# Turning the layer-1 weights through one ring of five buffers

## The chip, the cores and the metric

The kernel runs on one core of a Trainium2 chip. The metric is the device time of one execution, in microseconds. Before the change it is 4451.68 us, the median of three runs (4451.40 to 4455.35).

A core has a tensor engine (PE), a vector engine (DVE), a scalar engine (ACT), GpSimd (POOL) and a sync engine (SP). Each takes its instructions in a fixed order. Here SP issues plain loads and stores, and POOL issues gathers (indirect DMAs).

## The reference

The program is a two-layer model on `x` of 32 batches x 512 nodes x 256 features with an integer adjacency of 32 x 512 x 512. Each layer adds a graph step and then a feed-forward step to `x`:

```python
x = x + L0_gnn(layernorm(x), adj);  x = x + L0_ffn(layernorm(x))
x = x + L1_gnn(layernorm(x), adj);  x = x + L1_ffn(layernorm(x))
```

The feed-forward of layer 0 mixes a "tropical" product with a classical one:

```python
trop = max_d(x[:, None, :] + Wt[None]) + bt      # then piecewise linear
fused = g * trop + (1 - g) * gelu(x @ Wc + bc);  out = fused @ Wd + bd
```

The feed-forward of layer 1 projects the nodes softly onto 64 slices per head, runs a two-directional state-space mixer over the slices, and spreads the result back:

```python
fx = x @ W_fx.T;  sw = softmax((x @ W_x.T @ W_slice.T + b_slice) / temp)
zxbcdt = st @ hy_in_w.T;  ...  yg = yg * rsqrt(mean(yg ** 2)) * hy_norm_w
ot = yg @ hy_out_w.T;  out = spread(ot, sw) @ out_w.T + out_b
```

All weights of layer 1 come as rows (output by input). The kernel needs several of them turned, with the input dimension on the partitions.

## The kernel before

**Layer 0** (`layer0_sorted`, lines 98 to 704) handles the batches in four segments of eight. In a segment, 32 tiles of 128 rows make eight groups of four tiles. For a group, `sums` (L546 to L610) gathers the rows of four tiles (`xs`), transposes them (`xsp`, L577, into two PSUM banks tagged "tp"), and computes the tropical product by gathers. A row's result is the maximum over a short list of candidate features, each of which needs one gathered row of a table:

- the first candidate is gathered into `best` (L564), and ACT adds its value (L592);
- for tiles with more than eight candidates, DVE finds the list (`tops`, L585 to L589);
- each further candidate is a POOL gather of 512 KB (`rows`, L595) followed by a DVE maximum (L598). There are four `rows` buffers.

ACT then copies the transposed rows to `xnT` (L605). `mixed` (L613 to L643) does the classical half: per feature block the matmuls `clsp` and `gatep` (L623), ACT's functions `cls` and `gate` (L625), the transposes `tz` of `best` (L630), ACT's `acc` and `past` (L632, L636), and DVE's mixing (L637 to L641). `down` (L645 to L655) is the last matmul `po` (L652, 64 matmuls a group), a DVE addition and the store `x2s` by SP. The code interleaves the `mixed` of one group with the `sums` of the next.

In names such as `best_1_3` below, the first number is the group and the second the tile; for `clsp_0_5`, `tz_1_0` and the like, the group and the feature block. Group 7 is the last one of segment 2, groups 0, 1 and 2 are the first ones of segment 3. Pieces are called by their weight and row block: `in_0` is the first of `hy_in_w`.

**Layer 1** (`layer1_plain`, from L865) begins with a set-up that makes its turned weights. It is a Python generator: at each `yield` the program goes back to emitting layer-0 work. The set-up is thus interleaved with the last segment's feed-forwards, in the stretch from about 1849 to 2110 us of the profiled execution. A scheduler then settles the order of each engine from priorities and from its own estimates, and the engines run in that order. So the order in which the code is written and the order in which an engine runs it are not quite the same. A pool hands out buffers by tag: an instruction that needs a tile waits until the tile's earlier user is done.

The set-up before the change:

- `load_T` (L992 to L1004) takes a weight in pieces of 128 rows. For each, SP loads the piece into a raw buffer (L998), PE transposes its blocks of 128 columns into a "tp" PSUM bank (L1002), ACT copies the result into the turned weight (L1003). Raw buffers have one tag for each width with two buffers each. There are 21 pieces: `W_fx` 4 (256 columns, 128 KB each), `hy_in_w` 10 (512 columns, 256 KB each, the last one 16 rows), `hy_out_w` 4, `out_w` 2, `hy_fcD_w` 1. The "tp" banks are the same two that layer 0 uses for `xsp`.
- The norm weight is loaded (L1012), and DVE scales the turned `hy_out_w` (`hoT`) with it in four multiplications (L1014).
- `W_slice` is loaded twice and transposed (`twice_T`, L1016 to L1025); `W_x` (L1030), `b_x` (L1032) and `b_slice` (L1035) are loaded.
- Their products `wslp` (L1044), the scaled `wsl` (L1048), the bias row `bsl` (L1051 to L1055), its exponential `ebsl` (L1068), and bounds from the squares `wsl2` (L1060) follow.
- Then come the masks of batch 0 (L1073 to L1108): adjacency rows `ai` loaded by SP, `a` made by ACT, `maskp` transposed by PE.

Of the kernel before, what the change touches and what calls it, by code (L numbers as in the profile page):

```python
# [8 lines left out]
F32 = mybir.dt.float32  # L9
# [10 lines left out]
P = 128  # L20
N = 512
D = 256
# [842 lines left out]
def layer1_plain(tc, ident, eps, x2s, ranks, adj, w, out, over, ps):  # L865
# [3 lines left out]
    nc = tc.nc  # L869
# [31 lines left out]
    with ExitStack() as ctx:  # L901
# [3 lines left out]
        def ctile(name, shape):  # L905
            return cst.tile(shape, F32, tag=name, name=name)
# [6 lines left out]
        def psum(tag, name):  # L913
            return ps.tile([P, N], F32, tag=tag, name=name)
# [10 lines left out]
        with tc.tile_pool(name="raw0", bufs=1, side="right") as raw:  # L925
            prod = raw.tile([P, DC, AH, HO], F32, tag="prod", name="prod")
            norm2 = raw.tile([P, DC, 2, AH], F32, tag="norm2", name="norm2")
            for i, name in enumerate(("a_dst", "a_src")):
                dst = wa[:, :, AH * (HO + i) : AH * (HO + i + 1)]
# [51 lines left out]
        wfxT = ctile("wfxT", [P, DC, DI])  # L981
# [3 lines left out]
        inT = ctile("inT", [P, KC, DIN])  # L985
        hoT = ctile("hoT", [P, KC, DI])
        owT = ctile("owT", [P, KC, D])
        fcT = ctile("fcT", [P, KC, H])

        with tc.tile_pool(name="raw", bufs=2, side="right") as raw:  # L990

            def load_T(dst, src, name):  # L992

                R, Ccols = src.shape
                for r0 in range(0, R, P):
                    n = min(P, R - r0)
                    t = raw.tile([P, Ccols], F32, tag=f"raw{Ccols}", name=f"{name}_{r0}")
                    nc.sync.dma_start(t[:n], src[r0 : r0 + n, :])  # L998
                    pt = psum("tp", f"{name}p{r0}").rearrange("p (c r) -> p c r", r=P)
                    cs = Ccols // P  # L1000
                    for c in range(cs):
                        nc.tensor.transpose(pt[:, c, :n], t[:n, c * P : (c + 1) * P], ident[:n, :n])  # L1002
                    nc.scalar.copy(dst[:, :, r0 : r0 + n], pt[:, :cs, :n])  # L1003
                    yield  # L1004

            yield from load_T(wfxT, w["W_fx"], "wfx")
            yield from load_T(inT, w["hy_in_w"], "in")
            yield from load_T(hoT, w["hy_out_w"], "ho")
            yield from load_T(owT, w["out_w"], "ow")
            yield from load_T(fcT, w["hy_fcD_w"], "fc")  # L1010
            norm = raw.tile([P, KC], F32, tag="norm", name="norm")
            nc.sync.dma_start(norm, w["hy_norm_w"].rearrange("(c p) -> p c", p=P))  # L1012
            for c in range(KC):
                nc.vector.tensor_scalar_mul(hoT[:, c, :], hoT[:, c, :], norm[:, c : c + 1])  # L1014

            def twice_T(src, name):  # L1016

                R, Ccols = src.shape
                t = raw.tile([P, 2, Ccols], F32, tag="twice", name=name)
                for i in range(2):  # L1020
                    nc.sync.dma_start(t[:R, i, :], src)
                pt = psum("tp", f"{name}p")
                nc.tensor.transpose(pt[:, :R], t[:R].rearrange("p i c -> p (i c)"), ident[:R, :R])
                return pt


            wsT = raw.tile([P, G], F32, tag="wsT", name="wsT")
            nc.vector.tensor_copy(wsT, twice_T(w["W_slice"], "ws")[:, :G])
            wx = raw.tile([P, KC, D], F32, tag="wx", name="wx", bufs=1)
            nc.sync.dma_start(wx, w["W_x"].rearrange("(k p) d -> p k d", p=P))  # L1030
            bx = raw.tile([P, KC], F32, tag="bx", name="bx")
            nc.sync.dma_start(bx, w["b_x"].rearrange("(k p) -> p k", p=P))  # L1032
            bsl = raw.tile([1, H, G], F32, tag="bsl", name="bsl", bufs=1)
            bs = raw.tile([1, G], F32, tag="bs", name="bs")
            nc.sync.dma_start(bs, w["b_slice"].rearrange("(o n) -> o n", o=1))  # L1035
            for c in range(DC + 1):
                M = P if c < DC else 1
                for i in range(H // KC):

                    half = slice(i * C, (i + 1) * C)  # L1040
                    px = psum("mm", f"wslp{c}_{i}")
                    for k in range(KC):
                        lhs = wx[half, k, c * P : (c + 1) * P] if c < DC else bx[half, k : k + 1]
                        nc.tensor.matmul(px[:M, k * G : (k + 1) * G], lhs, wsT[half, :], start=True, stop=True)  # L1044
                    px = px[:M, : KC * G].rearrange("p (k g) -> p k g", k=KC)
                    rt = rtemp[:M, i :: H // KC].unsqueeze(2).to_broadcast([M, KC, G])
                    if c < DC:
                        nc.vector.tensor_mul(wsl[:, c, i :: H // KC, :], px, rt)  # L1048
                    else:
                        dst = bsl[:, i :: H // KC, :]  # L1050
                        nc.vector.tensor_add(dst, px, bs.unsqueeze(1).to_broadcast([1, KC, G]))  # L1051
                        nc.vector.tensor_mul(dst, dst, rt)
                yield
            wsl = wsl.rearrange("p c h g -> p c (h g)")
            nc.sync.dma_start(bsl_row.rearrange("(o n) -> o n", o=1), bsl.rearrange("p h g -> p (h g)"))  # L1055
            nc.sync.dma_start(ebsl, bsl_row.partition_broadcast(P))
            pn = psum("mm", "norm2s")
            for c in range(DC):
                sq = raw.tile([P, H * G], F32, tag="wsl2", name=f"wsl2_{c}")
                nc.vector.tensor_mul(sq, wsl[:, c, :], wsl[:, c, :])  # L1060
                nc.tensor.matmul(pn, ones, sq, start=c == 0, stop=c == DC - 1)
            most = raw.tile([P, 3], F32, tag="most", name="most")
            nc.vector.tensor_reduce(most[:, 0:1], pn, AX.X, ALU.max)
            nc.vector.tensor_reduce(most[:, 1:2], ebsl, AX.X, ALU.max)
            nc.vector.tensor_reduce(most[:, 2:3], ebsl, AX.X, ALU.min)
            for i, limit, op in ((0, SMALL_S, ALU.is_gt), (1, SMALL_B, ALU.is_gt), (2, -SMALL_B, ALU.is_lt)):
                nc.vector.tensor_scalar(over[:, 2 * AH + i : 2 * AH + i + 1], most[:, i : i + 1], limit, None, op)
            nc.scalar.activation(ebsl, ebsl, AF.Exp)  # L1068
# [1089 lines left out]
def tile_kernel(ctx, tc, ins, out):  # L2158
# [81 lines left out]
```

## Time and profile before

| | us |
|---|---|
| median of three runs | 4451.68 |
| lowest and highest run | 4451.40, 4455.35 |
| profiled execution, its own time | 4459.08 |
| span of the profiled execution | 4456.4 |
| PE busy (88% of the span) | 3922.0 |
| DVE busy (75%) | 3347.2 |
| ACT busy (51%) | 2291.6 |
| POOL busy (39%) | 1718.8 |

The mean granted TensorE clock is 0.948 of full speed. The profile is of one execution; times in microseconds count from the start of its span. In a line of waits, the numbers are the total, the times and the longest; in a timeline line, the start, the duration, the engine, the code line, the operation, the tiles written and read, and in brackets the idle time ahead of it with what ended it. "PE" rows are matmuls, "PEld" rows weight loads that overlap with them, "SPq" rows the DMA issues of SP.

### The profile page before, as it was taken

Reading aid. Unit: us, or ns where it says so; the run is one execution under the profiler, and the core shown is the slowest. Engines: PE = TensorE matmul, PEld = TensorE weight load, DVE = VectorE, ACT = ScalarE, POOL = GpSimd, SP = SyncE. Lnnn points to the kernel's source line nnn. Section 1 sums busy time; section 2 is a strip of 40 time slices with the busy share of each in tenths; the row PEclk is TensorE's granted clock in tenths of the full one; section 3 lists DMA queues with packets and bytes.
Section 4 is the critical chain, followed back from the end, with each engine's and each line's share of the span. In section 5 each row is a group of like instructions: output and inputs, shape, how many; then the busy total and the mean of one; then the engine's idle time right before and its main releaser. Section 6 shows DMA issues by size and latency. Waiting matters only on the chain.

```text
span 4456.4 us, 57911 instructions
## 1 busy us (share of the span) xinstructions
PE 3922.0 (88%) x20311; PEld 2470.6 (55%) x20311; DVE 3347.2 (75%) x7008; ACT 2291.6 (51%) x4756; POOL 1718.8 (39%) x2036
## 2 busy tenths in 40 slices
PE   5568898899988999888997899999999999999987
PEld 4454565566656656545554455555555555555555
DVE  6668887897788987877766777767677877778763
ACT  3345565566564665556654544544545444454433
POOL 2357644664446644454314232332222232332220
PEclk8679999999999999989998999999999999999998
DMA  5546543664436543564422111111111111111100
GB/s 133 160 144 223 190 130 122 210 200 139 156 117 213 187 147 129 162 201 167 138 81 67 36 53 57 56 48 58 51 43 42 53 55 55 58 48 58 41 15 16
DMA packets 235107, 474.21 MB, mean 106 GB/s; under 512 B 38299, under 2 KB 114075, under 8 KB 234804
## 3 DMA queue, kind: packets, MB, share of 16 engines
q0 software_dynamic: 98688, 315.94, 22.2%
q1 hardware_dynamic: 136116, 154.46, 11.0%
q8 instruction: 162, 2.65, 0.2%
q14 instruction: 141, 1.16, 0.1%
HBM read 413.16 MB, written 57.16 MB: 106 GB/s over the span
## 4 chain that ended last, share of the span: by engine, by line
DVE 34%; PE 32%; DMA 11%; issue 9%; POOL 9%; ACT 5%; SPq 0%; POOLq 0%; DVEq 0%; ACTq 0%
DVE att L1213 5%; DVE acc L637 4%; PE clsp L623 3%; PE avp L1249 3%; PE po L652 3%; PE gatep L623 3%; DMA rows<-table,xs 2%; PE yTp L1347 2%; DVE sw L1337 2%; DVE sw L1342 2%; DVE best L598 2%; DMA rows<-table,tops 2%; DVE sst L1340 2%; DMA best<-table,xs 2%; PE xp L1400 1%
## 5 line engine op out<-in xcount | busy, mean ns | idle before, releaser
L623 PE MATMUL clsp<-xnT,wc 128*128 128x512 f32 x1024 | 520.8, 627 | 49.7 <-ACT cls L625 37.6
L623 PE MATMUL gatep<-xnT,wg 128*128 128x512 f32 x1024 | 499.8, 607 | 10.5 <-ACT gate L625 7.7
L652 PE MATMUL po<-wd,acc 128*128 128x256 f32 x2048 | 455.4, 381 | 6.1 <-DVE acc L641 3.8
L1213 DVE SCALAR_TENSOR_TENSOR att<-own,other,mask 128x512 f32<-128x512 f32 x512 | 392.9, 796 | 79.0 <-DMA own<-ownd 79.0
L652 PEld LDWEIGHTS po<-wd,acc 128*128 128x128 f32 x2048 | 388.3, 191 | 72.1 <-issue 9.2
L598 DVE SCALAR_TENSOR_TENSOR best<-rows,xs,best 128x1024 f32<-128x1024 f32 x212 | 274.4, 1295 | 121.9 <-ACT best L592 76.4
L637 DVE SCALAR_TENSOR_TENSOR acc<-past,fld,acc 128x512 f32<-128x512 f32 x448 | 345.7, 775 | 24.9 <-ACT past L636 16.9
L632 ACT ACTIVATE acc<-tz,fld 128x512 f32<-128x512 f32 x256 | 198.8, 777 | 269.3 <-PE tz L630 240.1
L623 PEld LDWEIGHTS gatep<-xnT,wg 128*128 128x128 f32 x1024 | 196.0, 196 | 252.3 <-issue 197.9
L636 ACT ACTIVATE past<-tz,fld 128x512 f32<-128x512 f32 x448 | 291.4, 693 | 68.1 <-DVE acc L637 66.6
L1347 PE MATMUL yTp<-sw,x 128*128 128x512 f32 x512 | 264.6, 655 | 64.3 <-DVE sw L1342 59.6
L595 POOL DMA_INDIRECT rows<-table,xs x212 | 249.5, 1177 | 171.6 <-DVE best L598 119.0
L1249 PE MATMUL avp<-att,hv 128*32 128x512 f32 x2048 | 298.9, 607 | 5.6 <-DVE att L1213 5.6
L623 PEld LDWEIGHTS clsp<-xnT,wc 128*128 128x128 f32 x1024 | 181.5, 198 | 188.1 <-issue 111.8
L434 PE MATMUL pm<-h,adj 128*128 128x258 f32 (+1 forms) x1024 | 181.2, 324 | 99.9 <-DVE keep L427 33.7
L1300 POOL TENSOR_TENSOR mu<-mu,eps 128x16 f32<-128x16 f32 x32 | 111.6, 3487 | 391.1 <-DVE mu L1299 391.0
L1335 PE MATMUL lgp<-wsl,x4T 128*128 128x512 f32 x512 | 242.8, 613 | 15.7 <-ACT sw L1336 6.8
L1154 POOL DMA_INDIRECT x<-x2s,ranks x128 | 135.9, 1062 | 298.1 <-DVE att L1213 148.1
L625 ACT ACTIVATE gate<-gatep,fld 128x512 f32<-128x512 f32 x256 | 175.5, 685 | 142.6 <-PE gatep L623 123.8
L553 POOL DMA_INDIRECT xs<-rows_of,order x128 | 156.1, 1219 | 221.5 <-DVE acc L637 100.8
L1567 PE MATMUL outp<-v,swT 128*128 128x256 f32 x1024 | 227.6, 381 | 0.0
L625 ACT ACTIVATE cls<-clsp,fld 128x512 f32<-128x512 f32 x256 | 176.1, 688 | 93.9 <-PE clsp L623 55.6
(599 smaller groups left out, 8978.1 us busy)
## 6 DMA issues: line engine op xcount, KB each, us to landing
adj<-in_adj POOLq DMA_DIRECT2D x128, 256.0 KB
ai<-in_adj SPq DMA_DIRECT2D x128, 256.0 KB
own<-ownd SPq DMA_DIRECT2D x128, 256.0 KB
rows_of<-keep SPq DMA_DIRECT2D x32, 550.0 KB
x<-in_x SPq DMA_DIRECT2D x32, 512.0 KB
x2s<-xs SPq DMA_DIRECT2D x32, 512.0 KB
out<-x SPq DMA_DIRECT2D x32, 512.0 KB
rows<-table,xs POOLq DMA_INDIRECT x212
```

The costliest lines, as they stand in the source:

```text
L595: nc.gpsimd.indirect_dma_start(out=row, out_offset=None, in_=table, in_offset=bass.IndirectOffsetOnAxis(ap=idxs[:, k : k + 1].bitcast(U32) ...
L598: nc.vector.scalar_tensor_tensor(m, row, vals[:, k : k + 1], m, ALU.add, ALU.max)
L623: nc.tensor.matmul(pf, wf[:, c, f * P : (f + 1) * P], xnT[:, c, :], start=c == 0, stop=c == DC - 1)
L625: nc.scalar.activation(o, pf, fn, bias=fld[:, f, bf : bf + 1], scale=1.0 if fn == AF.Gelu else 0.5)
L636: nc.scalar.activation(r, z, AF.Relu, bias=fld[:, f, AT + b : AT + b + 1])
L637: nc.vector.scalar_tensor_tensor(y, r, fld[:, f, CH + b : CH + b + 1], y, ALU.mult, ALU.add)
L652: nc.tensor.matmul(po[:, i, :], acc[f][:, t * P : (t + 1) * P], wd[:, f, :], start=f == 0, stop=f == FC - 1)
L1213: nc.vector.scalar_tensor_tensor(e, own[h], other[:, j, h : h + 1], mask[:, j, :], ALU.max, ALU.mult)
L1249: nc.tensor.matmul(pv[p][k * HW : (k + 1) * HW, :], hv[:, j, h, e : e + HW], weighed[b, h, j], **ends)
L1335: nc.tensor.matmul(pf, xnT[:, c, t * P : (t + 1) * P], wsl[:, c, :], start=c == 0, stop=c == DC - 1)
L1347: nc.tensor.matmul(py, xn[:, t, c * P : (c + 1) * P], sw[:, t, :], start=t == 0, stop=t == NT - 1)
L1567: nc.tensor.matmul(po[:, :D], swT[:, k, t * P : (t + 1) * P], v[:, k, :], start=k == 0, stop=k == KC - 1)
```

## The change

The small operands `W_x`, `W_slice` (twice), `b_x` and `b_slice` are loaded first. The 21 pieces go through one tag, `piece`, of five buffers of 512 columns each. Before a piece is transposed, the load of the piece three places on is emitted, and three loads are emitted before the first transpose, followed by one more `yield`. The squares `wsl2` take their buffers from the same ring. The helper `twice_T` is written out in place. No operation is added or taken away.

In the order built for each engine the following has moved, between about 1840 and 2110 us; outside it, the order is the same:

- SP issues `W_x`, `W_slice`, `b_x`, `b_slice`, pieces 0 to 4, the norm weight, pieces 5 to 8, the store of group 6, pieces 9 to 20, then the store of group 7. Before, it was `W_fx` 0 and 1, `in_0` and `in_1`, the norm weight, the small operands, `W_fx` 2 and 3, the store of group 6, the remaining pieces, the store of group 7.
- On PE and ACT, `in_0` to `in_9`, `ho_0` to `ho_3` and `ow_0` stand in one stretch after the `xnT_0` copies; before, `in_0` stood before group 0's `xsp`, and the others were spread between the matmuls of `po_7`. `po_7` now follows them in one block, then `ow_1`; `fc`, the `W_slice` transpose and `wslp` come after the `xnT_1` copies.
- On ACT, the addition for `best_0_3` stands before the `xnT_0` copies.
- On DVE, the four multiplications of `hoT` by the norm stand between the searches that fill `tops_1_0`; before, they stood after them.
- On PE, `po_0` stands behind `tz_1_0` and `tz_1_1` of tile `best_1_3` and the mask transposes; before, it stood ahead of them.

```diff
-            def load_T(dst, src, name):
-                R, Ccols = src.shape
-                for r0 in range(0, R, P):
-                    n = min(P, R - r0)
-                    t = raw.tile([P, Ccols], F32, tag=f"raw{Ccols}", name=f"{name}_{r0}")
-                    nc.sync.dma_start(t[:n], src[r0 : r0 + n, :])
-                    pt = psum("tp", f"{name}p{r0}").rearrange("p (c r) -> p c r", r=P)
...
-                    nc.scalar.copy(dst[:, :, r0 : r0 + n], pt[:, :cs, :n])
-                    yield
-            yield from load_T(wfxT, w["W_fx"], "wfx")
-            yield from load_T(inT, w["hy_in_w"], "in")
...
+            wx = raw.tile([P, KC, D], F32, tag="wx", name="wx", bufs=1)
+            nc.sync.dma_start(wx, w["W_x"].rearrange("(k p) d -> p k d", p=P))
+            twice = raw.tile([P, 2, w["W_slice"].shape[1]], F32, tag="twice", name="ws", bufs=1)
+            for i in range(2):
+                nc.sync.dma_start(twice[:G, i, :], w["W_slice"])
+            bx = raw.tile([P, KC], F32, tag="bx", name="bx")
+            nc.sync.dma_start(bx, w["b_x"].rearrange("(k p) -> p k", p=P))
+            bs = raw.tile([1, G], F32, tag="bs", name="bs")
+            nc.sync.dma_start(bs, w["b_slice"].rearrange("(o n) -> o n", o=1))
+            pieces = [(dst, w[name], r0)
+                      for dst, name in ((wfxT, "W_fx"), (inT, "hy_in_w"), (hoT, "hy_out_w"), (owT, "out_w"),
+                                        (fcT, "hy_fcD_w"))
+                      for r0 in range(0, w[name].shape[0], P)]
+            def fetch(i):
+                _, src, r0 = pieces[i]
+                n = min(P, src.shape[0] - r0)
+                t = raw.tile([P, DI], F32, tag="piece", name=f"piece{i}", bufs=5)
+                nc.sync.dma_start(t[:n, : src.shape[1]], src[r0 : r0 + n, :])
+                return t
+            coming = [fetch(i) for i in range(3)]
+            yield
+            for i, (dst, src, r0) in enumerate(pieces):
+                if i + 3 < len(pieces):
+                    coming.append(fetch(i + 3))
+                n, cs = min(P, src.shape[0] - r0), src.shape[1] // P
+                pt = psum("tp", f"piecep{i}").rearrange("p (c r) -> p c r", r=P)
+                for c in range(cs):
+                    nc.tensor.transpose(pt[:, c, :n], coming[i][:n, c * P : (c + 1) * P], ident[:n, :n])
+                nc.scalar.copy(dst[:, :, r0 : r0 + n], pt[:, :cs, :n])
+                yield
             norm = raw.tile([P, KC], F32, tag="norm", name="norm")
             nc.sync.dma_start(norm, w["hy_norm_w"].rearrange("(c p) -> p c", p=P))
             for c in range(KC):
                 nc.vector.tensor_scalar_mul(hoT[:, c, :], hoT[:, c, :], norm[:, c : c + 1])
...
-                sq = raw.tile([P, H * G], F32, tag="wsl2", name=f"wsl2_{c}")
+                sq = raw.tile([P, H * G], F32, tag="piece", name=f"wsl2_{c}", bufs=5)
```

More of the change, by code (lines that the diff above doesn't have):

```diff
@@ L990, in layer1_plain @@
         with tc.tile_pool(name="raw", bufs=2, side="right") as raw:
-            def load_T(dst, src, name):
-                R, Ccols = src.shape
-                for r0 in range(0, R, P):
-                    n = min(P, R - r0)
-                    t = raw.tile([P, Ccols], F32, tag=f"raw{Ccols}", name=f"{name}_{r0}")
-                    nc.sync.dma_start(t[:n], src[r0 : r0 + n, :])
-                    pt = psum("tp", f"{name}p{r0}").rearrange("p (c r) -> p c r", r=P)
[L1000 to L1003, printed above, removed]
-                    yield
@@ L1006, in layer1_plain @@
-            yield from load_T(wfxT, w["W_fx"], "wfx")
-            yield from load_T(inT, w["hy_in_w"], "in")
-            yield from load_T(hoT, w["hy_out_w"], "ho")
-            yield from load_T(owT, w["out_w"], "ow")
-            yield from load_T(fcT, w["hy_fcD_w"], "fc")
+            wx = raw.tile([P, KC, D], F32, tag="wx", name="wx", bufs=1)
+            nc.sync.dma_start(wx, w["W_x"].rearrange("(k p) d -> p k d", p=P))
+            twice = raw.tile([P, 2, w["W_slice"].shape[1]], F32, tag="twice", name="ws", bufs=1)
@@ L1014, in layer1_plain @@
                 nc.vector.tensor_scalar_mul(hoT[:, c, :], hoT[:, c, :], norm[:, c : c + 1])
[L1016 to L1024, printed above, removed]
-            wsT = raw.tile([P, G], F32, tag="wsT", name="wsT")
[L1028 to L1032, printed above, removed]
+            pt = psum("tp", "wsp")
+            nc.tensor.transpose(pt[:, :G], twice[:G].rearrange("p i c -> p (i c)"), ident[:G, :G])
+            wsT = raw.tile([P, G], F32, tag="wsT", name="wsT")
+            nc.vector.tensor_copy(wsT, pt[:, :G])
             bsl = raw.tile([1, H, G], F32, tag="bsl", name="bsl", bufs=1)
-            bs = raw.tile([1, G], F32, tag="bs", name="bs")
-            nc.sync.dma_start(bs, w["b_slice"].rearrange("(o n) -> o n", o=1))
             for c in range(DC + 1):
```

## The prediction

> **What bounds the kernel now.** I read the page's busy times first, then the busy time by stretch around the edited code, then the waits of each engine there, the timeline of TensorE, and the chain that ended last. Page, part 1:
>
> ```profile
> PE 3922.0 (88%) x20311; PEld 2470.6 (55%) x20311; DVE 3347.2 (75%) x7008; ACT 2291.6 (51%) x4756; POOL 1718.8 (39%) x2036
> ```
>
> PE is the fullest engine, but that is an average. The edited code runs once, from 1849 us (its first load) to about 2010 us, beside the last feed-forwards of layer 0. By stretch:
>
> ```profile
> core 0: us, PE busy (x) PEld busy (x) DVE busy (x) ACT busy (x) POOL busy (x), PEclk, DMA share, GB/s
> 1895.00:1911.00 16.00, 14.91 (x50) 7.64 (x50) 16.00 (x19) 11.05 (x19) 11.26 (x10) 1.00 0.54 157
> 1911.00:1956.00 45.00, 33.88 (x140) 23.00 (x139) 28.45 (x41) 17.03 (x28) 20.36 (x18) 0.89 0.76 264
> 1956.00:2000.00 44.00, 39.22 (x145) 21.79 (x144) 33.73 (x52) 24.57 (x39) 20.26 (x20) 0.81 0.51 159
> 2000.00:2050.00 50.00, 42.44 (x154) 25.58 (x153) 42.65 (x56) 36.32 (x70) 26.87 (x22) 0.93 0.61 212
> ```
>
> In 1911 to 1956 no engine is full: PE idles 11.1 us of 45, DVE 16.5. This is where weight pieces are loaded and turned two at a time. SP's waits from 1845 to 1960, then DVE's waits from 1900 to 1960:
>
> ```profile
> SPq L998 <- PE inp L1002: 36.5, 8, 29.3
> SPq L998 <- DMA in<-in_L_ffn_hy_in_w: 15.3, 7, 4.1
> ```
>
> ```profile
> DVE hoT L1014 <- ACT hoT L1003: 11.1, 1, 11.1
> ```
>
> SP stood 29.3 us at one load, from 1882 to 1911, because both 512-wide buffers were full; then the loads came late. PE's timeline, and the chain that ended last:
>
> ```profile
> 1916.64 0.63 PE L1002 MATMUL inp<-ident,in 128*128 128x128 f32 x4 [1.92 <-DMA in<-in_L_ffn_hy_in_w]
> ...
> 1929.17 0.63 PE L1002 MATMUL inp<-ident,in 128*128 128x128 f32 x4 [2.91 <-DMA in<-in_L_ffn_hy_in_w]
> ...
> 1944.05 1.08 PE L1002 MATMUL hop<-ident,ho 128*128 128x128 f32 x4 [3.00 <-DMA ho<-in_L_ffn_hy_out_w]
> ```
>
> ```profile
> 1937.33 6.40 DMA rows<-table,tops
> 1943.77 8.70 issue
> 1952.69 0.93 POOL rows L595
> ```
>
> The chain shows what the late pieces cost. Rows for tile best_1_0 were gathered by 1943.8, but DVE stood at the norm scaling (L1014) until the last hoT copy, 1949.56. Its first maximum came at 1951.14, the next gather at 1952.69: the 8.70 us called issue. The edit can touch this, and nothing beyond 2110 us: the built order of each engine is the same there and before 1840 us.
>
> **What the Trainium skill says.** "PSUM — Partial Sum Buffer", Engine vs sequencer instructions, says that the queues of ScalarE, VectorE and GpSimdE are strict first in, first out. The trace agrees: DVE stood 11.1 us with rows for its next instruction there. "Perfetto Trace Analysis", Optimization Strategy, reads a repeated gap as possibly too few buffers for the next tile; SP's eight waits for inp agree. "DMA: Bandwidth & Descriptors", Issuing engines are not separate DMA queues, says that transfers from all issuers run on the same 16 engines and interleave: SP's pieces and POOL's gathers will compete. The trace has the share at 0.76 with both under way; it cannot show how a deeper ring divides it.
>
> **The change, part by part.** Instruction counts stay the same on every engine; only places and buffers change.
>
> *Small operands first.* W_x (512 KB), W_slice twice and the two biases go ahead of piece 0: five issues at the durations SP shows, 0.59 + 1.15 + 0.51 + 0.40, so piece 0 starts 2.7 to 3.1 us later. PE first stops for a piece at 1862.83 with a 4.36 us gap, and that gap is ACT's (its copy stands behind a layer-0 tile whose gather is late), so the delay fits under it: 0. If that gather were early it would cost up to 3.
>
> *Five buffers.* Load k now waits for the transposes of piece k-5. Pieces 0 to 3 are W_fx, turned at 1857 to 1881 as before, so pieces 5 to 8 (hy_in_w rows 1 to 4, 256 KB each) load at 1857 to 1882 rather than after 1881. That moves some 0.8 to 1 MB, 3 to 4 us of the 270 GB/s moved there, in among gathers. I put +1 (0 to +4). Layer 0's store x2s_6 stands behind pieces 7 and 8 on SP: at most 2.6 us later, with nobody waiting for it soon: 0.
>
> *The bunch.* hy_in_w piece 0 is no longer turned at 1881; fifteen pieces (in0 to in9, ho0 to ho3, ow0) now stand in one bunch on PE and ACT after the feed-forward's xsp transposes. Five are there at its start. The rest come five in flight; a load took 4.9, 5.3, 6.4, 6.6 and 5.7 us from issue to use before, so one each 1.1 to 1.3 us against 2.5 to 3 with two in flight. The bunch needs 15 x 0.6 = 9 us on PE and as much on ACT. I expect ten later pieces in 11 to 13 us, hidden in part by gate, cls and transposes between them, with 2.5 us of PE idle left of 11.1: -8.6 (-11 to -4).
>
> *ACT's order.* The bias of best_0_3 moved ahead of the two xnT_0 copies. It waits for its own gather; the copies, clsp_0 and the bunch wait behind it. A 512 KB gather took 6.3 to 7.9 us here and POOL now issues this one earlier, so part is covered: +3 (0 to +5).
>
> *PE's order.* po_7 (64 matmuls, 14 us) now follows the bunch unbroken; ow1 to ow3 and fc come after it, 4 x 0.6 = 2.4 us, into a stretch with 4.8 us idle (44 - 39.22): -2 on the path (-2.4 to 0). PE's sum: +1 - 8.6 + 3 - 2 = -6.6.
>
> *DVE's order.* The norm scaling now stands between the index searches of tops_1_0 rather than after them, so those gathers are queued behind four multiplies (1.67 us), and behind the hoT copies if these are late. The bunch should deliver ho3 by 1930 to 1936, before DVE gets there (1936 to 1938). Then gathers start about 1939.5 instead of 1937.33 and take 6.4: first maximum at about 1945.9 against 1951.14, -5.2. If ho3 came at 1941, the gain would be 2; at 1943.5 nothing.
>
> PE's -6.6 and DVE's -5.2 run side by side and feed each other (tz needs best, best needs gathers); the joint lead is near -6.
>
> *After 1990.* po_0 moved behind the masks and behind tz_1_0 and tz_1_1, which wait for ACT's best_1_3 and its gather. Before, this matmul hid waits:
>
> ```profile
> 2010.77 0.38 PE L630 MATMUL tz<-ident,best 128*128 128x128 f32 x2
> 2010.99 13.98 PE L652 MATMUL po<-wd,acc 128*128 128x256 f32 x64
> ...
> 2034.34 3.78 PE L623 MATMUL clsp<-xnT,wc 128*128 128x512 f32 x4 [5.50 <-ACT cls L625]
> ```
>
> With cover gone the gather is exposed for some 4 us (0 to +9); but the 5.50 us idle behind it, when ACT stood for ai (5.37 us) and DVE's acc, should shrink by as much, since po_0 now lies there: -4.5 (-5.5 to 0). Together -0.5.
>
> Squares in the ring's buffers, the removed helper functions, the additional yield: same instructions, 0; what the yield moves is in the orders above.
>
> Sum: -6 - 0.5 = -6.5. The profiled execution took 4459.08 us, 2.7 over its 4456.4 span and 7.4 over the median 4451.68. The stretch is a small part of it, so I carry the difference over whole: 4452.6 for a profiled run, 4445.2 for the median. About 0.2% (8.9 us) is what a measurement of this kernel can tell from no change.
>
> **Rivals.**
>
> *Absorbed.* Gathers set the pace from 1900 to 1965 and faster pieces only slow them. For: 16 DMA engines are 0.76 busy, and the chain's first item after issue is the gathers (22.9% of 1895 to 1985). Against: they idled around 1935 to 1938 and 1946 to 1950. The 1.5 MB of pieces pulled into 1914 to 1930 would delay two gathers by 2 to 3 us each: about -1, 4450.7.
>
> *Slower, by the exposed gather.* Tiles best_0_3 and best_1_3 each stand at the head of a queue with nothing behind to hide them. A full 6.3 to 7.9 us gather for each, less the 6 gained: 2 x 7.1 - 6 = +8; 4460, or up to 4466 if hoT is late too. It decides when best_1_3's gather lands more than about 8 us after PE has finished tz_0_7, so that the gap exceeds what the 5.50 us gap gives back. For: POOL's waits for DVE of 10.68 and 11.95 us show gather issue is often late. Against: gathers of a whole tile also moved forward with DVE.
>
> *Full return.* Both 11.1 us waits go, hidden neither by ACT nor by later gathers, and the 5.50 us gap too, with the 2.5 us of load waits that I leave standing: -(11.1 - 2.5 + 5.5) = -14.1, 4437.6. For: PE-bound from 2050 on, so every lead lasts. Against: the two waits overlap in time.
>
> **How the numbers follow.** Lead kept, 0.47 (own range 4438 to 4449, about half of it beyond 8.9 us if the errors lean to gain): 0.25 faster, 0.22 same. Full return 0.13, faster. Absorbed 0.15, same. Slower 0.25, of which 0.18 beyond 8.9 us and 0.07 within. Together 0.38, 0.44, 0.18. The range reaches from the full return's 4433 to the exposed gather's 4463, leaving 0.1 at each end.
>
> **What would show it.** SP's 29.3 us wait gone and pieces 4 to 8 in hand at 1914; inp and hop waits on DMA under 3 us; hoT L1014 not waiting, first best_1_0 maximum near 1946; po_7 ending near 1949 rather than 1956.3; a new ACT wait of about 3 us at best_0_3, and a PE wait for ACT's best_1_3 of about 4 us before po_0; every later stage shifted by one constant. It is wrong if hoT L1014 still waits over 5 us, if the lead at 1956 is gone by 2050, or if gathers lengthen beyond 9 us.

## The result, and the profile after

The changed kernel took 4446.67 us (median of 22 runs), the kernel before 4456.85 us in runs beside it (22). The ratio of the means is 0.9973, with a 95% interval of 0.9962 to 0.9984: 12 us faster, between 7 and 17 (the medians lie 10.2 us apart). The forecast of 6.5 us had the right sign and lies just under that interval; the case it belonged to (3 to 14 us) holds the measured value.

The profiled execution's span is 4430.7 us, against 4456.4 us before. Part 1 of the page after:

```profile
PE 3896.7 (88%) x20311; PEld 2459.0 (55%) x20311; DVE 3349.7 (76%) x7008; ACT 2294.0 (52%) x4756; POOL 1713.9 (39%) x2036
```

The instruction counts are those of before, and DVE, ACT and POOL are busy for the same time within 5 us. PE is busy for 25.3 us less, with the same matmuls. That was nowhere in the prediction, and it is taken up below: it is the clock that PE was granted. Over the whole span, a clock below full took 233.9 us before and 207.3 us after (the span times 1 - mean granted clock).

Busy time in two of the stretches, after (columns: stretch, length, busy time and instruction count of PE, PEld, DVE, ACT and POOL, granted clock, share of the DMA engines, GB/s):

```profile
1911.00:1956.00 45.00, 37.50 (x166) 25.73 (x165) 35.16 (x48) 23.72 (x40) 23.31 (x21) 0.92 0.79 281
1956.00:2000.00 44.00, 39.65 (x165) 20.65 (x164) 41.52 (x64) 28.96 (x50) 25.59 (x21) 0.96 0.62 196
```

From 1911 to 1956 PE idles 7.5 us instead of 11.1, and DVE 9.8 instead of 16.5. From 1956 to 2000 the clock is 0.96 where it was 0.81, and DVE gets 41.5 us of work done where it got 33.7.

SP's waits (1845 to 1960), then DVE's (1900 to 1960), after:

```profile
SPq L1013 <- PE piecep L1024: 60.8, 12, 34.8
```

```profile
DVE xs L654 <- PE po L652: 7.0, 2, 6.3
```

SP still stands at a load, for 34.8 us, but now with five pieces in hand. DVE hardly waits for hoT (0.3 us). It waits 6.3 us for something else: the addition of `po_7`, which stands ahead of the first maximum of best_1_0.

PE's timeline after (start, duration, what, and in brackets the idle time before it):

```profile
1922.62 0.63 PE L1024 MATMUL piecep<-ident,piece 128*128 128x128 f32 x4 [2.54 <-DMA piece<-in_L_ffn_hy_in_w]
...
1941.65 8.80 PE L652 MATMUL po<-wd,acc 128*128 128x256 f32 x40
```

The 2.54 us ahead of the first row are a wait for the very load at which SP had stood. The last row is the end of `po_7`, at 1950.45, where before it was at 1956.47.

One execution drifts against another by several microseconds over 4450. Distances inside the trace are steadier (within 2.2 us in two profiles of the changed kernel), so the experiments are read by four of them. Each is counted from SP's store of group 5, whose place in the order the change does not touch, and they run to the stores of groups 7, 0 and 1 and to the first output store. The fifth column is the time that PE lost to a low clock between 1840 and 2130 us: the sum over stretches of 2 us of 2 x (1 - granted clock).

| kernel | to group 7 | group 0 | group 1 | first output | lost to clock | ratio to before (95%) |
|---|---|---|---|---|---|---|
| before | 133.1 | 207.9 | 259.4 | 758.8 | 22.1 | 1 |
| changed | 125.5 | 200.4 | 247.3 | 745.2 | 8.5 | 0.9973 (0.9962 to 0.9984) |
| changed, again | 125.7 | 198.9 | 246.1 | 743.0 | 6.8 | 0.9952 (0.9934 to 0.9970) |
| small operands first | 132.5 | 209.6 | 262.3 | 759.2 | 20.9 | 0.9994 (0.9981 to 1.0007) |
| before, scale late | 137.5 | 215.2 | 268.4 | 767.2 | 23.9 | 1.0011 (1.0000 to 1.0021) |
| depth only | 127.2 | 200.0 | 250.4 | 748.5 | 17.1 | 0.9974 (0.9962 to 0.9985) |
| changed, three buffers | 125.4 | 201.4 | 249.1 | 746.7 | 6.8 | 0.9967 (0.9953 to 0.9982) |
| changed, two buffers | 134.0 | 208.9 | 257.5 | 753.8 | 19.3 | 0.9988 (0.9972 to 1.0003) |
| changed, no extra yield | 122.8 | 198.0 | 248.3 | 744.0 | 10.2 | 0.9973 (0.9961 to 0.9985) |
| changed, scale late | 126.4 | 201.0 | 248.8 | 747.7 | 10.1 | 0.9967 (0.9956 to 0.9978) |
| changed, without 12 loads | 122.0 | 194.5 | 243.4 | 741.2 | 13.7 | 0.9971 (0.9959 to 0.9983) |
| before, wslp first | 142.9 | 216.3 | 266.5 | 764.9 | 22.2 | 1.0004 (0.9991 to 1.0017) |
| before, busy matmuls | 132.0 | 208.4 | 263.7 | 760.5 | 15.3 | 1.0021 (1.0012 to 1.0030) |

The lead of 13.6 us at the first output shows at two of the stores. By the store of group 7 it is 7.6 us. Between the stores of groups 0 and 1 it grows again: that stretch takes 46.9 us instead of 51.5. From group 1 to the first output, before and after take 499.4 and 497.9 us, which is within what repeats.

But the stores do not stand at the same point of PE's work. In the changed kernel, six of the 512-column matmuls `clsp` and `gatep` (0.43 us each) that ran ahead of the end of `po_7` run behind it, and `po_0` stands behind six more of them than before. So 2.6 us of the first lead, and 2.6 of the 4.6 us between groups 0 and 1, are a matter of place. From the end of `po_5` to the end of `po_1`, PE has the same number of matmul records, 847, in all kernels of the table but the last (863, with the added ones). There its time can be divided in three: idle; the part of its busy time that a low clock took (busy time x (1 - granted clock)); and the rest.

| kernel | end of po_5 to end of po_1, us | PE idle | busy time lost to clock | rest |
|---|---|---|---|---|
| before | 258.6 | 33.5 | 20.1 | 205.0 |
| small operands first (order of before) | 261.1 | 36.9 | 18.3 | 206.0 |
| depth only | 249.4 | 29.8 | 13.4 | 206.1 |
| changed | 247.8 | 31.7 | 9.3 | 206.8 |
| changed, again | 245.8 | 31.3 | 6.4 | 208.1 |
| changed, three buffers | 248.9 | 34.7 | 6.0 | 208.2 |
| changed, two buffers | 257.3 | 36.3 | 14.6 | 206.4 |
| changed, without 12 loads | 242.9 | 27.5 | 9.5 | 205.9 |

The rest is nearly the same everywhere, as it should be for the same work. Against before, the changed kernel's two profiles are 10.8 and 12.8 us shorter: PE's loss to a low clock is 10.8 and 13.7 us smaller, and its idle time only 1.8 and 2.2 us (the rest is 1.8 and 3.1 longer). Against the second row, which has the order of before, clock and idle time give 9.0 and 5.2 us, and 11.9 and 5.6. So the greater part of the gain is PE's clock, and the waits are the smaller part.

### The profile page after: what moved, and what is told of

It reads as the page before. It is cut to its first block, busy times and chain, and to the rows that moved or that the text cites. A ratio compares the mean times of both kernels' runs of the same rounds, so it can differ in the third digit from the quotient of the medians.

```text
span 4430.7 us, 57926 instructions
## 1 busy us (share of the span) xinstructions
PE 3896.7 (88%) x20311; PEld 2459.0 (55%) x20311; DVE 3349.7 (76%) x7008; ACT 2294.0 (52%) x4756; POOL 1713.9 (39%) x2036
## 4 chain that ended last, share of the span: by engine, by line
PE 23%; DVE 19%; POOL 6%; DMA 4%; issue 3%; ACT 3%; DVEq 0%; POOLq 0%; SPq 0%; ACTq 0%
DVE att L1214 5%; PE avp L1250 3%; DVE sw L1338 2%; PE yTp L1348 2%; PE clsp L623 2%; DVE sw L1343 2%; DVE sst L1341 2%; PE gatep L623 2%; PE xp L1401 1%; PE oTp L1536 1%; PE zp L1394 1%; POOL x L1155 1%; PE adp L1255 1%; POOL hv L1190 1%; PE po L652 1%
## 5 line engine op out<-in xcount | busy, mean ns | idle before, releaser
L434 PEld LDWEIGHTS pm<-h,adj 128*128 128x128 f32 x1024 | 152.6, 214 | 123.7 <-issue 68.0
```

The source lines that it names most:

```text
L434: nc.tensor.matmul(pm[:, : c1 - c0], a[:, i, t * P : (t + 1) * P], h[:, i, c0:c1], start=i + c0 == 0, stop=i + 1 == NT and c0 > 0)
```

## The experiments

### The changed kernel again

> The changed kernel once more, to see how far its distances repeat. From SP's store of group 5 to that of group 7 it took 125.5 us (before: 133.1), to the store of group 0 200.4 (207.9), to that of group 1 247.3 (259.4), to the first output store 745.2 (758.8). If these leads (7.5, 7.5, 12.1, 13.6) are the change's, they repeat within 2 us; if the last two are drift between executions, they do not.

The distances repeat: 125.7, 198.9, 246.1 and 743.0 us, all within 2.2 us of the first profile. The leads are the change's and not drift.

### Only the small operands first

```diff
+            wx = raw.tile([P, KC, D], F32, tag="wx", name="wx", bufs=1)
+            nc.sync.dma_start(wx, w["W_x"].rearrange("(k p) d -> p k d", p=P))
...
+            nc.sync.dma_start(bs, w["b_slice"].rearrange("(o n) -> o n", o=1))
             yield from load_T(wfxT, w["W_fx"], "wfx")
```

> Only the small operands moved ahead of the first piece; the orders of PE, DVE, ACT and POOL are those of before. Theory (ring and orders make the gain): nothing, 133 +-1.5 us from the store of group 5 to that of group 7, 758.8 +-3 to the first output store, ratio 1.000. Rival (the small loads ahead matter): 130 or less to group 7, or 136 or more if the delay of piece 0 by 3 us is not covered.

132.5 and 759.2 us, ratio 0.9994. Nothing, as forecast: the 3 us by which the first piece comes later are covered.

### Before, with the scaling of hoT out of DVE's way

The norm weight is loaded and used after the squares. Its load waits for `W_x`'s buffer, so that the four multiplications can't come before the last `wslp`:

```diff
-            norm = raw.tile([P, KC], F32, tag="norm", name="norm")
-            nc.sync.dma_start(norm, w["hy_norm_w"].rearrange("(c p) -> p c", p=P))
-            for c in range(KC):
-                nc.vector.tensor_scalar_mul(hoT[:, c, :], hoT[:, c, :], norm[:, c : c + 1])
...
+            norm = raw.tile([P, KC, D], F32, tag="wx", name="norm", bufs=1)[:, :, 0]
+            nc.sync.dma_start(norm, w["hy_norm_w"].rearrange("(c p) -> p c", p=P))
+            for c in range(KC):
+                nc.vector.tensor_scalar_mul(hoT[:, c, :], hoT[:, c, :], norm[:, c : c + 1])
```

> Before, with the norm weight loaded and hoT scaled only after the squares (some 40 us later); the loads and turns stay two at a time. It takes DVE's 11.1 us wait away and leaves PE's 11 us of load waits. Theory (the gathers' head start counts only with PE's own lead): gathers of best_1_0 start near 1945 instead of 1952.7, po_7 ends where it did: 132 to 133 us to the store of group 7, 203 to 206 to group 0, 752 to 757 to the first output. Rival (DVE's wait alone carried the loss): as the changed kernel or better, 197 to 201 to group 0 and 745 to the first output.

Both theories missed. The kernel got no faster: 137.5 us to group 7 and 767.2 to the first output are later than before, and the ratio is 1.0011. DVE's waits from 1930 to 1960, and ACT's timeline:

```profile
DVE best L598 <- ACT best L592: 10.4, 1, 10.4
```

```profile
1953.19 0.59 ACT L1003 COPY hoT<-hop 128x512 f32<-128x512 f32 x1 [3.30 <-PE hop L1002]
1953.67 1.15 ACT L592 ACTIVATE best<-best,tops 128x1024 f32<-128x1024 f32 x1
```

The 11.1 us wait did not go; it changed its name. The first maximum of best_1_0 also needs ACT's addition to best_1_0 (L592), and that stood behind the third hoT copy on ACT. In the trace of before the same addition stands right behind a copy that waited 3.50 us for the piece:

```profile
1945.17 0.58 ACT L1003 COPY hoT<-hop 128x512 f32<-128x512 f32 x1 [3.50 <-PE hop L1002]
1945.65 1.15 ACT L592 ACTIVATE best<-best,tops 128x1024 f32<-128x1024 f32 x1
```

So the late pieces held this tile up on two engines at once, and DVE's wait was only the one that ended last. The Trainium skill ("PSUM — Partial Sum Buffer", Engine vs sequencer instructions) names ACT among the engines with a strict first-in, first-out queue, and the trace agrees: the addition starts at 1953.67, behind a copy that began at 1953.19 after a wait of 3.30 us.

Why it is even later by 4.4 us at group 7 was not settled. PE's waits for pieces came to 11.3 us against 9.1, and one for a gate to 1.80 against 1.26; these make up 2.7 of it, and one profile can't tell chance from the edit.

### Depth alone, in the code of before

```diff
-                    t = raw.tile([P, Ccols], F32, tag=f"raw{Ccols}", name=f"{name}_{r0}")
+                    t = raw.tile([P, Ccols], F32, tag=f"raw{Ccols}", name=f"{name}_{r0}",
+                                 bufs=4 if Ccols == DI else 2)
...
-                sq = raw.tile([P, H * G], F32, tag="wsl2", name=f"wsl2_{c}")
+                sq = raw.tile([P, H * G], F32, tag="raw512", name=f"wsl2_{c}", bufs=4)
```

> Before, with four buffers for the 512-column pieces (the squares share them to make room); the loads stay where they were written, one piece at a time, small operands after. Theory (the order follows the depth: with free buffers the scheduler bunches the turns and moves wsp as in the changed kernel): 125 to 128 us to the store of group 7, 743 to 748 to the first output, ratio 0.997. Rival (the early fetch and the small loads are needed too): 131 to 133 and 757 to 759.

127.2 and 748.5 us, ratio 0.9974. The theory holds: two more buffers, with no load written earlier, bring 10.3 of the 13.6 us, and the ratio is that of the changed kernel. The scheduler makes its order from the buffers; DVE's order around `tops_1_0` came out as in the changed kernel.

### The ring's depth in the changed kernel's order: three and two

```diff
-                t = raw.tile([P, DI], F32, tag="piece", name=f"piece{i}", bufs=5)
+                t = raw.tile([P, DI], F32, tag="piece", name=f"piece{i}", bufs=3)
...
-            coming = [fetch(i) for i in range(3)]
+            coming = [fetch(i) for i in range(1)]
...
-                if i + 3 < len(pieces):
-                    coming.append(fetch(i + 3))
+                if i + 1 < len(pieces):
+                    coming.append(fetch(i + 1))
```

The cut shows three buffers; the run with two has `bufs=2`. The buffers of the squares go with them.

> The changed kernel with three buffers and loads emitted one piece ahead; the engines' orders are those of the changed kernel but for 61 matmuls of PE and 16 instructions of ACT. Theory (depth feeds the bunch): three pieces in hand at its start instead of five, three in flight after that, the last hoT copy near 1943 instead of 1936.5: 130 to 133 us to the store of group 7, 203 to 207 to group 0, 750 to 757 to the first output. Rival (the order alone brings the gain): 125.5 and 745 like the changed kernel.

Three buffers: 125.4 and 746.7 us. The rival holds, and my theory falls: the fourth and fifth buffers are worth at most 1.5 to 3.7 us at the first output, about what repeats. PE did wait longer for pieces in the bunch (1905 to 1960):

```profile
PE piecep L1024 <- DMA piece<-in_L_ffn_hy_in_w: 7.9, 5, 2.9
```

With 0.2 us more at `hy_out_w` that is 8.1 us against 4.6 in the changed kernel, and nearly the 9.1 of before. What differs from before is where the waits fall: at `hy_in_w`, and no longer at `hy_out_w`, whose copies stand ahead of the gathered tile on ACT (the changed kernel itself waits 2.1 us there). That this is what counts is not shown: to the end of `po_1` PE idles 34.7 us with three buffers, no less than before, and what is gained is clock (6.0 us of busy time lost instead of 20.1).

> The changed kernel with two buffers and loads emitted one piece ahead: the depth of before, in nearly the changed kernel's order. Three buffers gave the changed kernel's time. Theory (order first, depth matters only below some number): with two in flight a piece comes each 2.5 to 3 us, ten after the bunch's start take 25 to 30 us, so ho3 lands near 1948 as before: 131 to 136 us to the store of group 7, 752 to 760 to the first output. Rival (order alone is enough at any depth): 126 and 745.

Two buffers: 134.0 and 753.8 us, as the theory said.

```profile
PE piecep L1024 <- DMA piece<-in_L_ffn_hy_in_w: 8.6, 5, 3.9
PE piecep L1024 <- DMA piece<-in_L_ffn_hy_out_w: 3.6, 2, 3.4
```

The waits at `hy_out_w` are back, and the whole first lead is gone (133.1 before). From group 0 to group 1 it takes 48.6 us (before 51.5, changed 46.9), and here too `po_0` stands so that 2.6 us of this are a matter of place. So the first lead needs the third buffer.

### Without the extra yield

```diff
             coming = [fetch(i) for i in range(3)]
-            yield
```

> The changed kernel without the additional yield after the first three loads; SP's order stays, the other engines' orders shift in this stretch. Theory (depth and the bunch behind the feed-forward make the gain, the yield only moves where it begins): 125 to 128 us to the store of group 7, 743 to 749 to the first output, under 12 us lost to a low PE clock between 1840 and 2130. Rival (the order that the yield gives is needed): 130 or more, 752 or more, and over 16 us lost.

122.8 (better than either expectation), 198.0 and 744.0 us; ratio 0.9973. The yield is worth nothing that shows here. In this order, and in that of depth alone, as many `clsp` and `gatep` run between `po_0` and `po_1` as before, and from group 0 to group 1 it takes 50.3 and 50.4 us: without the change of place, little of a second lead is left.

### The changed kernel with the scaling late

The same edit as in the late scaling of before.

> The changed kernel with hoT scaled only after the squares, as in scale-late. The four multiplications (1.7 us) leave the searches of tops_1_0, so the gathers of best_1_0 can start 1 to 1.7 us earlier. Theory (they are no longer what DVE waits for: the addition of po_7 stands ahead of the first maximum and waited 6.3 us): 124.5 to 127 us from the store of group 5 to that of group 7, 198 to 201 to group 0, 742 to 747 to the first output. Rival (the gathers still set the pace): 122 to 124, and 738 to 741.

126.4, 201.0 and 747.7 us: no gain, as the theory had it. DVE's waits from 1930 to 1960:

```profile
DVE xs L654 <- PE po L652: 8.7, 2, 8.1
```

The 1.7 us of the multiplications went into DVE's wait for `po_7` (8.1 us, 6.3 in the changed kernel). The gathers of best_1_0 did not start earlier, as both expectations had it: they began 112.6 us after the store of group 5, and 112.5 and 112.6 in the changed kernel.

### The changed kernel without its later loads

```diff
             def fetch(i):
+                if i > 8:
+                    return coming[4 + i % 5]
```

> The changed kernel without the loads of pieces 9 to 20: those turns read pieces 4 to 8 again (so most of the turned weights are not the right ones). All other instructions and every order are those of the changed kernel. It bounds what any ring can still bring. Theory (loads are no longer on the path): PE's 4.6 us of waits for loads go, first maximum of best_1_0 1 to 3 us earlier, po_7 3 to 4 us earlier; 121 to 124 us from the store of group 5 to that of group 7, 741 to 744 to the first output, ratio to the changed kernel 0.999. Rival (loads still hold gathers and PE up): 118 or less and 737 or less.

122.0 and 741.2 us, as the theory said: with all 12 later loads gone, 3.5 us are left at group 7 and 2 to 4 at the first output, and the ratio to before does not differ from the changed kernel's. PE waits for no piece any more, but stands 6.0 us for a gate, because ACT waited 9.29 us for the gather of best_0_3:

```profile
1917.40 1.15 ACT L592 ACTIVATE best<-best,xs 128x1024 f32<-128x1024 f32 x1 [9.29 <-DMA best<-table,xs]
```

So no deeper ring can bring more than these few us.

### The clock: wslp somewhere else, and matmuls that keep PE busy

PE was granted half its clock for 17 us in before. The same stretch of time, before and then after:

```profile
1970.00:1988.00 18.00, 16.32 (x64) 10.41 (x65) 11.53 (x22) 8.65 (x15) 7.77 (x8) 0.54 0.27 79
```

```profile
1970.00:1988.00 18.00, 18.00 (x86) 9.32 (x85) 17.48 (x28) 7.27 (x13) 9.50 (x8) 1.00 0.41 112
```

PE is busy nearly all of the time in both, but with 64 instructions in one and 86 in the other. In before, 16 matmuls of wslp take 2.88 us, after 1.60 us. Just ahead of the slow stretch, before has three PE gaps of 0.91, 0.88 and 1.79 us around xsp and wsp.

The Trainium skill has this, and the prediction did not use it: "TensorE: Matmul & The Clock Gate", What's actually happening, says that PE's clock is halved unless PE has been busy lately, that it falls after an idle window of about 3.4 us and comes back after a busy one, and that the windows run on their own. The traces agree on the windows. The clock is 1.00 or 0.50, and in each of the twelve profiles of the runs above (all but the last in the table) all its changes lie on one grid of 3.413 us that runs through the execution; so what a dip costs comes in steps of 1.7 us. They differ on what counts as idle. I took PE's busy share in every window of this grid. At full clock, the clock fell after all 688 windows with under 40% busy, after 138 of 1032 with 40 to 70%, and after none of 12268 with more. So less than a fully idle window is enough. At half clock, it never came back after a window with under 80% busy (636), and it came back after 722 of 741 with 90% or more. Of the other 19, 12 hold wslp.

In the first run, the pieces are loaded and turned after the `W_slice` transpose and wslp, which so come earlier:

```diff
-            yield from load_T(wfxT, w["W_fx"], "wfx")
...
             def twice_T(src, name):
...
+            yield from load_T(wfxT, w["W_fx"], "wfx")
...
             wsl = wsl.rearrange("p c h g -> p c (h g)")
```

> Before, with the W_slice transpose and wslp moved ahead of the pieces (they then run near 1860 us); loads and turns still two at a time. Before, small-first and scale-late each showed PE at half clock for 16 us or more from wsp on (about 1971 to 1988, or 10 us later), just after a cluster of gaps of 0.9 to 1.8 us around wsp; the changed kernel showed none there. Theory (the gaps around wsp set the clock back, and half of the change's gain is that stretch at full clock): no half-clock stretch after xnT_1, the distance from the store of group 7 to that of group 1 (before: 126.3 us; changed: 121.7) falls to about 119 to 122, ratio near 0.998. Rival (the clock falls there whatever stands there, or the gain is the earlier gathers): the half-clock stretch stays, 125 to 127 us, ratio 1.000.

The theory was half right. The long slow stretch after xnT_1 is gone (one dip of 1.7 us is left), but the distance from group 7 to group 1 fell only to 123.5 us, and the kernel gained nothing: from 1840 us to the store of group 7, 11.9 us were lost to the clock (8.5 before). Where wslp stands now, PE meets a gap and goes slow again:

```profile
1866.24 1.60 PE L1034 MATMUL wslp<-wsT,wx 64*128 64x64 f32 x16
1870.83 2.07 PE L623 MATMUL clsp<-xnT,wc 128*128 128x512 f32 x2 [2.99 <-ACT xnT L605]
1872.83 2.88 PE L1034 MATMUL wslp<-wsT,wx 64*128 64x64 f32 x16
```

The same 16 matmuls take 1.60 us ahead of a 2.99 us gap and 2.88 behind it. So the low clock moved and did not go. Nor is its loss worth its full length at its old place: some 4 us of wslp (1.60, 1.60 and 0.83 at full clock) and 5 us of clock loss (11.9 before, 7.0 here) left the stretch from group 7 to group 1, for 2.8 us. On PE itself, `po_7` to `po_1` took 7.1 us less, and 4.5 us of this were gone again by the end of `po_2`.

Then the clock by itself:

```diff
+            wm = psum("mm", "busy")
+            for _ in range(8):
+                nc.tensor.matmul(wm[:G], wsT, hoT[:, 0, :], start=True, stop=True)
             bsl = raw.tile([1, H, G], F32, tag="bsl", name="bsl", bufs=1)
```

> Before, with eight matmuls of 64 x 512 put between the W_slice transpose and wslp; their result is not used. In before, PE ran at half clock from wsp on for 17 us (8.4 us lost) though it was busy for 16.3 of 18 us, with wslp of 64 x 64 and transposes for the most part. Theory (a stretch of idle or of small matmuls and transposes sets the clock to half, a stretch of full-width matmuls sets it back): the clock is full again within 4 to 7 us of their start, 3 to 5 us lost in this stretch; the added 3.4 us at full clock (6.8 at half) and the clock won cancel, 125 to 128 us from the store of group 7 to that of group 1 (before 126.3), ratio 1.000. Rival (the clock does not follow PE's work of the last microseconds): still 8 us or more lost there, 130 us or more.

PE's timeline behind the same gap of 1.79 us:

```profile
1976.87 0.27 PE L1023 MATMUL wsp<-ident,ws 64*128 64x64 f32 x1 [1.79 <-ACT xnT L605]
...
1979.25 9.64 PE L1035 MATMUL busy<-hoT,wsT 128*64 128x512 f32 x16 [0.77 <-DVE wsT L1028]
1988.82 1.60 PE L1047 MATMUL wslp<-wsT,wx 64*128 64x64 f32 x16
```

The clock dropped at the gap as before, and was full again some 5 us after the added matmuls began, with 3.4 us lost instead of 8.5. wslp then ran in 1.60 us. So what PE does sets its clock: matmuls of 512 columns without a break brought it back, while wslp of 64 x 64, transposes and a few clsp did not in 17 us, although PE was busy all the time in four of the five windows of that stretch. I had priced the added matmuls too low. They show as 16 passes and took 9.64 us, not 3.4 to 6.8, so that group 7 to group 1 took 131.7 us (the rival's number, for another reason), and the kernel was slower by 0.2%. As a cure it costs more than it saves.

## Why the prediction was right, point by point, and where by luck

**The direction and the first lead** were right, but not by the sum that was put down for them. PE's waits for pieces from 1905 to 1960, before and then after:

```profile
PE inp L1002 <- DMA in<-in_L_ffn_hy_in_w: 6.1, 4, 2.9
PE hop L1002 <- DMA ho<-in_L_ffn_hy_out_w: 3.0, 1, 3.0
```

```profile
PE piecep L1024 <- DMA piece<-in_L_ffn_hy_in_w: 2.5, 1, 2.5
PE piecep L1024 <- DMA piece<-in_L_ffn_hy_out_w: 2.1, 2, 1.7
```

They fell from 9.1 to 4.6 us, so where the term of -8.6 stood for these waits, -4.5 came (7.0 us were left in the second profile). And the waits did not turn into a lead. From the end of `po_6` to the end of `po_7` PE idles 12.4 us before, 12.4 after and 12.3 in the second profile, because its waits for ACT grew from 3.5 to 7.8 us (5.4 in the second). Counted from the end of `po_5`, `po_7` ended 6.3 and 6.8 us earlier; 2.6 us of this are the six matmuls that moved behind it, PE's idle time gave 0.5 and 0.1 us, and what is left is for the most part low clock, for which the prediction had no term. That the forecast of 6 us met the first lead was largely luck.

**PE's order, -2:** the size was near, the reading was not. There are two `ow` pieces and no `ow2` or `ow3`, and `fc` stood behind `po_7` before as well. What moved behind it were the six matmuls `clsp` and `gatep`, 2.6 us, and the last transpose of `ow_1`.

**Small operands first, 0:** right, shown by the run with nothing else.

**Five buffers, +1 us:** no such loss is in the trace; group 5 to group 6 took 55.6 us against 57.0, and of the gathers whose landing shows, none came near the 9 us that the prediction named as a sign: best_0_3's took 5.6 us at most, from its issue at 1906.84 to ACT's addition at 1912.40, and the longest on the chain that ended last 6.38. But the number five was given too much weight: three give the same.

**"SP's 29.3 us wait gone":** wrong. It is 34.8 us, and costs PE 2.54 us for that piece. A load that waits for a buffer is late only when PE gets to its piece before it has landed, and then by that much.

**ACT's order, +3:** of the right size at this place. ACT waited 5.33 us for best_0_3's gather at 1912.40, and PE 1.87 us behind it. In all, PE's waits for ACT grew by 4.3 us up to `po_7`.

**DVE's order, -5.2:** the first maximum came at about 1947.3 us, against a forecast of 1945.9 and 1951.14 before: -3.9. The step read the chain wrongly. "DVE stood at the norm scaling until the last hoT copy" is true, but ACT's addition stood behind the hoT copies too, and taking DVE's wait away alone gained nothing. In before the rows had landed by 1943.8 and the addition ended at 1946.80, so at most the last 4.3 us before 1951.14 were the scaling's, and not 11.1. The first maximum is now behind the addition of `po_7`, which the prediction did not list among what DVE would meet next, though it stood one place behind it in the order of before.

**After 1990, -0.5:** both terms were wrong. It was +4 for the exposed gather of best_1_3 and -4.5 for the gap behind po_0. The gather was not exposed at all: PE's waits from 1990 to 2060 after are

```profile
PE gatep L623 <- ACT gate L625: 4.1, 1, 4.1
PE maskp L1085 <- ACT a L1094: 2.6, 2, 1.7
PE gatep L623 <- ACT cls L625: 2.1, 1, 2.1
```

with none for a tz. The gap behind po_0 shrank from 5.50 to 4.12 us, less than I had put. And yet the lead grew by 4.6 us from group 0 to group 1. Of this, 2.6 us are the later place of `po_0`, which the prediction saw only as a loss of cover. The rest is of the size of what the clock took less between the ends of `po_0` and `po_1` (1.7 us) and PE idled less (1.3 us).

**A term that was missing, and the largest: the clock.** Between 1840 and 2130 us PE lost 22.1 us to a low clock before, and 8.5 and 6.8 us in the two profiles after. The 17 us at half clock from 1971 are gone, 8.5 us alone. The kernels with two buffers lie at 19 or more, but for the one with added matmuls (15.3). Those made from the changed kernel with three or more lie at 14 or less. By the division of PE's time above, the clock is 9 to 14 us of the 11 to 15 us by which the changed kernel leads at the end of `po_1`, and the waits, which the prediction was about, are 2 to 6. What full clock alone would bring is not shown by this: depth alone lost 17.1 us and gained 10.3, and where wslp moved, the low clock moved with it.

**The rivals:** *Absorbed* fell, since the DMA engines were 0.79 busy and the lead stood. *Slower, by the exposed gather* fell for best_1_3. For best_0_3 the wait is real (5.33 us on ACT, 9.29 without the loads), and 1.87 and 6.0 us of it reached PE. *Full return*, -14.1, was nearer to the measured 12 us than the case I chose, though its reason was not the one at work: both waits were not returned, and new ones (6.3 us at `po_7`, 4.12 us at a gate) took part of their place.

## What to carry to other kernels

When waits are to be removed, check on the engine that is to gain whether its idle time fell in all: here 4.5 us of load waits went and as much waiting for another engine came, and what was gained was clock. Look at everything the waiting instruction needs and not only at the releaser that came last: here the same late load stood ahead of it on two engines, and removing one showed only the other. In a ring of loads, more buffers help up to a number: two were too few here and three as good as five, with loads of 5 to 6.6 us, and a run that leaves the loads out shows what is left to win. And price a PE gap at more than its length: add the microseconds at half clock that may follow, above all where small matmuls and transposes come after it.

## What was not expected of the hardware

PE's clock falls after much less than a fully idle stretch: it fell after each of 688 windows of 3.413 us in which PE was busy for under 40%, and after none of 12268 with over 70%. In before it then stayed at 0.50 for 17 us while PE was 91% busy with 64 x 64 matmuls, transposes and few wider ones, and came back some 5 us after matmuls of 512 columns began in the same place. Between two profiles with the same instruction counts, PE's busy time differs by 25.3 us, and the spans by 25.7 us; part of that lies outside the changed stretch (low-clock loss from 2130 to 4400 us: 71.7 us before, 60.7 after), where the order is the same, so that it is drift between executions and not the change.
